# First norm of batches 3 to 7 from x loaded channels first, its factors by way of DRAM; first and last group norm by halves, spread by TensorE; new turns

## The chip, the core and the metric

The kernel runs on one NeuronCore of a Trainium2 chip. Its engines are TensorE (PE in the profile; its weight loads are PEld), VectorE (DVE), ScalarE (ACT), GpSimd (POOL) and SyncE (SP), which here only issues DMAs. The metric is the device time of one execution in microseconds; less is better.

## What is computed

One RWKV block over x of 8 batches, 256 tokens and 512 channels, all in float32, cut to what matters here:

```python
xn = ln(x, ln1_w, ln1_b)                      # first norm, over the 512 channels of a token
sx = shift(xn) - xn                           # the token before, less the token itself
xxx = tanh((xn + sx * maa_x) @ maa_w1)        # 5 groups of 32
x5 = xn + sx * (maa + xxx @ maa_w2)           # five mixtures
w = exp(-exp(time_decay + tanh(x5[1] @ decay_w1) @ decay_w2))
r, k, v = x5[3] @ Wr.T, x5[0] @ Wk.T, x5[2] @ Wv.T
g = silu(x5[4] @ Wg.T)
for t in tokens:                              # 32 heads of 16 x 16
    a = k[t][:, None] * v[t][None, :]
    out[t] = r[t] @ (u * a + s)
    s = a + w[t][:, None] * s
att = group_norm(out) * gn_w + gn_b           # over the 16 channels of a head
x = x + (att * g) @ Wo.T
xn2 = ln(x, ln2_w, ln2_b); sx2 = shift(xn2) - xn2
xk, xr = xn2 + sx2 * ffn_maa_k, xn2 + sx2 * ffn_maa_r
out = x + sigmoid(xr @ ffn_Wr.T) * (square(relu(xk @ ffn_Wk.T)) @ ffn_Wv.T)
```

## The kernel before

Each batch passes three stages: `inputs_of_scan` (first norm, mixtures, projections k, v, r, g), `scan` (the recurrence, one scan instruction of VectorE over 4 x 256 elements, 16 of them a batch) and `rest` (group norm, Wo, second norm, feed-forward). Activations lie channels first: 128 channels by 256 tokens, two such blocks to a tile.

`Plan` records every operation with an engine, a guessed duration and its buffers, and `order` lays them out: an operation with a lower rank goes first where it can start. The ranks are the table `TURNS` (lines 127 to 263), one row for each stage of each batch; `LANDS`, `WAY` and the others are guesses of DMA times that enter the layout only. What reaches the chip is a fixed order of instructions on each engine. All loads and stores but those of v go out on SP's queue in that order, and an instruction that waits holds up all behind it on its queue.

Names that matter:

- The first norm of batches 2 to 7 (`normed`, lines 592 to 641): two ScalarE passes over each of two token tiles sum x and its squares (L595, L599), GpSimd makes the factor by a power (L634), ScalarE scales the tile (L638), and `turned` has TensorE turn it in 8 transposes (L658) into PSUM, from where ScalarE applies the weight and bias (L681). GpSimd takes the shift difference `sx` (L690).
- The scan (`scan`): v goes to DRAM (`vo`) and comes back spread over partitions (`vs<-vo`, 128 DMAs of 512 KB into 6 buffers), is multiplied by k (L1001, or on GpSimd L998), scanned (L1003, into `st`), multiplied by r on GpSimd (L1006) and summed over partitions by TensorE (L1014, "the gather", 16 matmuls of a quarter of the array's columns each).
- The group norm (`rest`, lines 1029 to 1086): squares (L1032), means of squares by four matmuls (L1040, into a quarter of the columns each), a square root (L1045), a reciprocal on VectorE (L1051). For batches 0 to 6 the 32 rows that result are spread to 128 partitions by 16 ScalarE copies (L1073), and GpSimd multiplies (L1076); for batch 7 TensorE spreads them (L1059) and VectorE multiplies (L1067). Then weight and bias (L1080), the gate (L1085 or L1083) and Wo.
- The second norm of batches 0 to 6 makes its mixtures with `between`: two scaled copies on ScalarE (L729, L734), added on GpSimd (L736).
- ScalarE's functions lie in sets; `tables` puts a table load (L1170) where the next function is not in the set that is loaded.
- TensorE instructions come in forms: the full array ("128*128"), a quarter of the columns ("128*32", four side by side), a quarter or a half of the rows ("32*128", "64*128"), and transposes. Where several are side by side, one row of the profile holds them all.

```python
act(256, rs, [pv, eh], lambda: nc.scalar.activation(
    rs()[:, 0:T], pv()[:, 0, :], AF.Sqrt, bias=eh()[:, 0:1]), "sqrt", 1)
...
    dve(256, [rs], [rs], lambda: nc.vector.reciprocal(rs()[:, 0:T], rs()[:, 0:T]), 6.25)
```

Of the kernel before, what the change touches and what calls it, by code (L numbers as in the profile page):

```python
# [12 lines left out]
P = 128  # L13
# [55 lines left out]
class Plan:  # L69
# [5 lines left out]
    LANDS = {"vs__": (2.3, 2.45), "s": (0.3, 2.4), "vo_": (0.7, 2.2), "vo__": (0.35, 2.0), "o_": (0.7, 1.2), "x": (1.8, 2.3),  # L75
             "xt": (1.7, 2.0), "xs": (0.7, 0.9), "idt": (0.2, 1.6), "Wfk_": (1.7, 2.7), "Wfr_": (1.7, 2.7),
             "Wfv_": (1.7, 2.7), "Wo_": (1.7, 2.7)}
    WAY = 1.4
    TABLES = {"exp": "exp_and_others", "tanh": "exp_and_others", "silu": "silu_and_others", "sig": "sigmoid_and_others",
              "sqrt": "sqrt_and_others"}  # L80
# [16 lines left out]
    def add(self, engine, us, outs, ins, emit, mode=None, into=(), lag=0.0, kb=0, part=False):  # L97
# [3 lines left out]
        if kb:  # L101
            op.wire, op.lag = self.LANDS.get("".join(c for c in op.bufs[0].name if not c.isdigit()), (kb / 308, 1.7))

# [17 lines left out]
    def stage(self):  # L121
# [258 lines left out]
def tile_rwkv_block(  # L380
# [133 lines left out]
    def load(buf, src, kb):  # L514
        dma(buf, lambda: src, buf, kb)
# [730 lines left out]
```

## Time and profile before

| | |
|---|---|
| median of 3 runs | 608.0 us (607.12 to 609.82) |
| span of the profiled execution | 607.4 us |
| busy: DVE | 539.7 us (89%) |
| busy: ACT | 519.0 us (85%) |
| busy: POOL | 511.6 us (84%) |
| moved by DMA | 124.73 MB, mean 205 GB/s |

The profile shows one execution and gives no time of its own but the span, from the first to the last instruction; the median of the runs lies 0.6 us above it. Busy times are sums over an engine's instructions, shares are of the span. A row of groups names line, engine, operation, tiles out and in, count, then busy time, mean length of one, and the idle time just before, with what ended it. A row of a window gives its length, each engine's busy time with its instructions, and the clock granted to TensorE as a share of full speed.

### The profile page before, as it was taken

How to read it: one execution, taken by the hardware profiler on the slowest of the kernel's cores; microseconds unless marked ns; L12 is line 12 of the kernel's file. 1: busy time of each engine (PE TensorE's matmuls, PEld its weight loads, DVE VectorE, ACT ScalarE, POOL GpSimd, SP SyncE). 2: the span in 40 equal slices, each digit the busy share in tenths (PEclk: the TensorE clock that was granted, in tenths of full speed). 3: DMA queues.
4: the chain of work that ended last, by engine and by line, in shares of the span. 5: the costliest groups of instructions: out<-in, count | busy, mean ns of one | idle time of the engine just before them, and what ended most of it. 6: DMA issues, size and time to landing. Idle time of an engine off the chain costs nothing.

```text
span 607.4 us, 17029 instructions
## 1 busy us (share of the span) xinstructions
PE 596.5 (98%) x7022; PEld 346.3 (57%) x7022; DVE 539.7 (89%) x492; ACT 519.0 (85%) x1177; POOL 511.6 (84%) x405
## 2 busy tenths in 40 slices
PE   9999998899999999999999999999999999999997
PEld 7575655347634774446654584465744474546464
DVE  5789999799999999998899999999899999995342
ACT  5977879979999999989999999999998899968350
POOL 2989999989979999899989899988889798987020
PEclk9999999799999999999999999999999999999999
DMA  9887695649668789669767987788667878972352
GB/s 316 272 198 209 184 253 170 167 119 284 193 162 227 198 250 244 182 191 253 202 196 214 269 215 213 210 256 216 166 184 195 231 202 216 282 206 74 130 187 77
DMA packets 52638, 124.73 MB, mean 205 GB/s; under 512 B 5841, under 2 KB 11345, under 8 KB 52561
## 3 DMA queue, kind: packets, MB, share of 16 engines
q1 hardware_dynamic: 48048, 119.39, 70.3%
q10 hardware_dynamic: 4512, 4.26, 2.2%
q8 instruction: 55, 0.90, 0.7%
q14 instruction: 23, 0.18, 0.1%
HBM read 115.25 MB, written 8.39 MB: 204 GB/s over the span
## 4 chain that ended last, share of the span: by engine, by line
PE 68%; POOL 14%; ACT 7%; DVE 5%; DMA 3%; issue 2%; SPq 0%; ACTq 0%; DVEq 0%; POOLq 0%
PE ps L440 57%; POOL st L1006 7%; PE ps L1014 7%; POOL mix L822 3%; PE ps L658 2%; POOL vs L998 1%; DVE st L1003 1%; DMA vo<-v 1%; PE ps L862 1%; PE ps L564 1%; DMA x<-in_x 1%; DMA vs<-vo 1%; DVE vs L1001 1%; ACT xh L595 1%; POOL mix L850 1%
## 5 line engine op out<-in xcount | busy, mean ns | idle before, releaser
L1003 DVE TENSOR_TENSOR_SCAN st<-wrep,vs 128x1024 f32<-128x1024 f32 x128 | 287.9, 2273 | 7.1 <-PE ps L1014 3.5
L1006 POOL TENSOR_TENSOR st<-st,r 128x1024 f32<-128x1024 f32 x128 | 254.8, 2008 | 7.4 <-DVE st L1003 6.0
L1001 DVE TENSOR_TENSOR vs<-vs,ps 128x1020 f32<-128x1020 f32 x122 | 142.6, 1199 | 2.0 <-ACT ps L980 1.0
L440 PE MATMUL ps<-Ws,mix 128*32 128x512 f32 (+3 forms) x872 | 115.1, 585 | 0.0
L440 PEld LDWEIGHTS ps<-Ws,mix 128*32 128x32 f32 (+1 forms) x872 | 37.5, 116 | 63.1 <-issue 58.5
L822 POOL TENSOR_TENSOR mix<-mix,xn 128x512 f32<-128x512 f32 x62 | 66.9, 1103 | 4.1 <-DVE mix L806 4.0
L1014 PE MATMUL ps<-st,con 128*32 128x256 f32 x1024 | 63.7, 388 | 2.4 <-POOL st L1006 1.6
L440 PE MATMUL ps<-mix,Wv 128*32 128x256 f32 (+1 forms) x832 | 59.5, 380 | 1.2 <-DVE mix L819 1.0
L440 PE MATMUL ps<-mix,Wk 128*32 128x256 f32 (+1 forms) x856 | 59.8, 380 | 0.0
L440 PE MATMUL ps<-mix,Wr 128*32 128x256 f32 (+1 forms) x712 | 59.2, 380 | 0.0
L440 PE MATMUL ps<-mix,Wg 128*32 128x256 f32 (+1 forms) x544 | 58.1, 380 | 0.1
L440 PE MATMUL ps<-Ws,g 128*32 128x512 f32 (+1 forms) x416 | 58.1, 606 | 0.0
L440 PE MATMUL ps<-mix,Ws 128*32 128x256 f32 (+1 forms) x688 | 57.8, 380 | 0.0
L1014 PEld LDWEIGHTS ps<-st,con 128*32 128x32 f32 x1024 | 33.1, 111 | 30.0 <-issue 9.0
L440 PEld LDWEIGHTS ps<-mix,Wg 128*32 128x32 f32 (+1 forms) x544 | 42.2, 133 | 12.8 <-issue 0.7
L440 PEld LDWEIGHTS ps<-mix,Wv 128*32 128x32 f32 (+1 forms) x832 | 36.6, 116 | 22.4 <-issue 3.0
L440 PEld LDWEIGHTS ps<-mix,Ws 128*32 128x32 f32 (+1 forms) x688 | 39.6, 123 | 16.7 <-issue 1.4
L440 PEld LDWEIGHTS ps<-mix,Wr 128*32 128x32 f32 (+1 forms) x712 | 38.8, 122 | 16.9 <-issue 1.3
L440 PEld LDWEIGHTS ps<-mix,Wk 128*32 128x32 f32 (+1 forms) x856 | 37.0, 115 | 19.8 <-issue 2.2
L804 ACT ACTIVATE ps<-ps,vec 128x256 f32<-128x256 f32 x112 | 45.5, 448 | 2.9 <-PE ps L440 2.0
L1170 ACT ACT_TABLE_LOAD x33 | 42.3, 1283 | 0.6
L736 POOL TENSOR_TENSOR mix<-mix,sx 128x512 f32<-128x512 f32 x28 | 35.5, 1279 | 6.6 <-ACT mix L729 3.7
(143 smaller groups left out, 1000.4 us busy)
## 6 DMA issues: line engine op xcount, KB each, us to landing
vs<-vo SPq DMA_DIRECT2D x128, 512.0 KB, 5.2
Ws<-in_wo SPq DMA_DIRECT2D x16, 512.0 KB, 5.4
Ws<-in_fk SPq DMA_DIRECT2D x16, 512.0 KB, 5.5
Ws<-in_fr SPq DMA_DIRECT2D x16, 512.0 KB, 5.7
Ws<-in_fv SPq DMA_DIRECT2D x16, 512.0 KB, 5.3
x<-in_x SPq DMA_DIRECT2D x9, 512.0 KB, 6.0
vo<-v ACTq DMA_DIRECT2D x15, 256.0 KB, 5.4
out<-o SPq DMA_DIRECT2D x15, 256.0 KB, 3.8
```

The lines of the kernel that those rows point to most:

```text
L440: nc.tensor.matmul(out[i : i + n], lhsT=w[:, i : i + n], rhs=x, start=first, stop=final)
L564: nc.tensor.matmul(ps()[:, 0, :], lhsT=warm[:, 0, 0:P], rhs=warm[:, 0, 0:T], start=True, stop=True)
L595: summed(junk[n], mv, [src[n]], lambda n=n: nc.scalar.activation(junk[n](), src[n](), AF.Copy, accum_out=mv()[:, n, 0:1]), 0)
L658: nc.tensor.transpose(to[:, m, n * P : (n + 1) * P], xh[n]()[:, k * P : (k + 1) * P], idt())
L736: gp(512, t, [t, u], lambda t=t, u=u: nc.gpsimd.tensor_tensor(t(), t(), u(), ALU.add))
L804: act(256, p_, [p_, vec], lambda g=g, q=q, m=m, p_=p_: nc.scalar.activation(p_()[:, m, :], p_()[:, m, :], AF.Identity, bias=col(f"maa_{g}" ...
L822: gp(512, t, [t, xn[q]], lambda q=q, t=t: nc.gpsimd.tensor_tensor(t(), t(), xn[q]()[:, :, 1 : T + 1], ALU.add))
L1001: dve(4 * T, [vs], [vs, kp], lambda m=m, vs=vs, kp=kp: nc.vector.tensor_tensor(vs()[:, :, 1:T], vs()[:, :, 1:T], kp()[:, m : m + 1, 1:T].t ...
L1003: dve(4 * T, [st], [w, vs, first], lambda w=w, vs=vs, st=st: nc.vector.tensor_tensor_scan(st().rearrange("p n t -> p (n t)"), w().rearrang ...
L1006: gp(4 * T, st, [st, r], lambda m=m, st=st, r=r: nc.gpsimd.tensor_tensor(st(), st(), r()[:, m : m + 1, :].to_broadcast([P, 4, T]), ALU.mul ...
L1014: nc.tensor.matmul(pat()[32 * i : 32 * i + 32, 0, :], lhsT=con()[:, s : s + 32], rhs=done[i]()[:, j, :], start=(j == 0), stop=(j == 3),)
L1170: nc.scalar.preload_act_table_set(op.table)
```

## The change

- **First norm of batches 3 to 7.** The host passes x a second time with channels first (`x_turned`). The sums over x stay as they were. GpSimd makes the factor and minus mean times factor (`rn`), one DMA writes these 2 x 256 numbers to DRAM (`bd`), one reads them back spread over all 128 partitions (`bc`). ScalarE copies the factor row into PSUM, two DMAs bring x channels first straight into `xn`, VectorE multiplies, GpSimd adds, ScalarE applies weight and bias in place. The two scalings L638, the 8 transposes and their way out of PSUM are gone for these batches.
- **Group norm.** Square root and reciprocal become a logarithm and an exponential of -1/2 of it, both on ScalarE, in one set of functions that other exponentials may use too. In batches 0 and 7 each half of the channels has its own means, logarithm, exponential and spreading by TensorE, and VectorE multiplies; so batch 0 loses its 16 copies and both GpSimd multiplications.
- **Smaller.** The second scaled copy of `between` lies one element further in its tile. The weights `mw2b` and `dw2` are passed without repeats.
- **Turns.** All ranks and the guesses of DMA times are new.

```diff
-    LANDS = {"vs__": (2.3, 2.45), "s": (0.3, 2.4), "vo_": (0.7, 2.2), "vo__": (0.35, 2.0), "o_": (0.7, 1.2), "x": (1.8, 2.3),
...
-    WAY = 1.4
+    LANDS = {"vs__": 2.33, "s": 0.4, "vo_": 0.85, "vo__": 0.25, "o_": 0.8, "x": 1.55, "xt": 1.5, "xs": 0.9, "idt": 0.2,
...
+    WAY, LANDED = 1.18, 1.15
-              "sqrt": "sqrt_and_others"}
+              "sqrt": "sqrt_and_others", "ln": "natural_log_exp_and_others"}
...
     TURNS = """
-        8 72 12 20 41 124 40 135 48 116 79 78 141 119 3 32 84 31 128 181 183 185 11 10 19 39 62 68 36 65 69 37
+        8 80 3 54 31 46 105 114 69 103 123 75 126 116 1 4 27 113 106 108 111 112 33 5 41 49 52 53 34 45 73 43
...
+            elif want == "exp" and mode == "ln":
+                want = mode
...
+        "sx": lambda t: t[:, 0 : 2 * T].rearrange("p (m t) -> p m t", m=2),
...
+        spread = which == 1 and b > 2
...
+        if spread:
+            return turned_by_host(mn, rs, row, b)
...
+    def turned_by_host(mn, rs, row, b):
+        u, i = f"1_{b}", NVEC + 2 * b + row
+        rn, there, bc, rsb = new("rn", f"rn{b}"), new("bd", f"bd_{b}"), new("bc", f"bc{b}"), new("ps", f"rsb{b}")
+        gp(2, rn, [rs, eh], lambda: nc.gpsimd.tensor_tensor(rn()[:, 0, :], rs(), eh()[:, 2:4], ALU.pow), 340)
+        gp(2, rn, [mn, rn], lambda: nc.gpsimd.tensor_tensor(rn()[:, 1, :], mn(), rn()[:, 0, :], ALU.mult), 30)
+        dma(there, lambda: rn(), lambda: there().rearrange("w (n p) -> p w n", p=P), 2, rn)
+        dma(bc, lambda: there().unsqueeze(0).to_broadcast([P, 2, T]), bc, 262, there)
+        act(256, rsb, [bc], lambda: nc.scalar.copy(rsb()[:, 0, :], bc()[:, 0, :]))
+        xns, sxs = [], []
+        for q in range(NQ):
+            xn, sx = new("xn", f"xn{u}_{q}"), new("sx", f"sx{u}_{q}")
+            dma(xn, lambda q=q: x_turned[b, 2 * q * P : (2 * q + 2) * P, :].rearrange("(m p) t -> p m t", p=P),
+                lambda xn=xn: xn()[:, :, 1 : T + 1], 262)
...
+            dve(512, [xn], [xn, rsb], lambda xn=xn: nc.vector.tensor_tensor(
+                xn()[:, :, 1 : T + 1], xn()[:, :, 1 : T + 1], rsb()[:, 0:1, :].to_broadcast([P, 2, T]), ALU.mult))
+            gp(512, xn, [xn, bc], lambda xn=xn: nc.gpsimd.tensor_tensor(
+                xn()[:, :, 1 : T + 1], xn()[:, :, 1 : T + 1], bc()[:, 1:2, :].to_broadcast([P, 2, T]), ALU.add))
+            for m in range(2):
+                k = 2 * q + m
+                act(256, xn, [xn, vec], lambda m=m, k=k, xn=xn: nc.scalar.activation(
+                    xn()[:, m, 1 : T + 1], xn()[:, m, 1 : T + 1], AF.Identity, bias=col("ln1_b", k), scale=col("ln1_w", k)), pointers=2)
...
-            u = new("sx", f"u{name}_{q}")
+            u = Buf("sx", f"u{name}_{q}", lambda t: t[:, 1 : 2 * T + 1].rearrange("p (m t) -> p m t", m=2))
...
+        split = b == 0 or last
+        if split:
+            pr = []
+            for q, sq in enumerate(sqs):
+                pv, half = new("ps", f"pv{b}_{q}"), slice(64 * q, 64 * q + 64)
...
+                pe(0.437, [pv], [con, sq], mm, "columns")
+                act(256, sq, [pv, eh], lambda sq=sq, pv=pv, half=half: nc.scalar.activation(
+                    sq()[half, 0:T], pv()[half, 0, :], AF.Ln, bias=eh()[half, 0:1]), "ln", 1)
+                act(256, sq, [sq], lambda sq=sq, half=half: nc.scalar.activation(
+                    sq()[half, 0:T], sq()[half, 0:T], AF.Exp, scale=-0.5), "ln")
+                p_ = new("ps", f"psr{b}_{q}")
...
+                        nc.tensor.matmul(p_()[:, m, :], lhsT=con()[half, s : s + P], rhs=sq()[half, 0:T], start=True, stop=True)
...
-            dve(256, [rs], [rs], lambda: nc.vector.reciprocal(rs()[:, 0:T], rs()[:, 0:T]), 6.25)
...
+            act(256, rs, [rs], lambda: nc.scalar.activation(rs()[:, 0:T], rs()[:, 0:T], AF.Exp, scale=-0.5), "ln")
```

How the order of instructions moves is shown at three places. A row gives line, operation and tiles (`_` and a number is the buffer), then the shape of the output.

The first place is GpSimd around the gate of batch 0's group norm. Before, the last of 20 products `st` of the scan stands behind the two multiplications by the spread factors (`att<-att,sq` and `att<-att,rk`), and the gate (`g<-att,g`) behind that:

```order
L998 TENSOR_TENSOR vs_149<-vs_149,k_127 128x4x255
L1006 TENSOR_TENSOR st_156<-st_156,r_128 128x1024
L1006 TENSOR_TENSOR st_159<-st_159,r_128 128x1024
L1076 TENSOR_TENSOR att_141<-att_141,sq_162 128x2x256
L1076 TENSOR_TENSOR att_142<-att_142,rk_153 128x2x256
L1006 TENSOR_TENSOR st_155<-st_155,r_128 128x1024
L1085 TENSOR_TENSOR g_138<-att_141,g_138 128x512
L1085 TENSOR_TENSOR g_137<-att_142,g_137 128x512
```

Now the gate of one half stands ahead of the last four of the same 20 products and that of the other just behind them:

```order
L1137 TENSOR_TENSOR g_140<-att_143,g_140 128x512
L1047 TENSOR_TENSOR st_162<-st_162,r_132 128x1024
L863 TENSOR_TENSOR mix_117<-mix_117,xn_105 128x512
L863 TENSOR_TENSOR mix_119<-mix_119,xn_104 128x512
L1047 TENSOR_TENSOR st_160<-st_160,r_132 128x1024
L1039 TENSOR_TENSOR vs_152<-vs_152,k_129 128x4x255
L1047 TENSOR_TENSOR st_164<-st_164,r_132 128x1024
L1047 TENSOR_TENSOR st_161<-st_161,r_132 128x1024
L1137 TENSOR_TENSOR g_139<-att_144,g_139 128x512
```

The two multiplications are gone from GpSimd, and the gates have moved ahead; the kinds of work up to the 20th product are otherwise the same in number.

The second place is TensorE where batch 0's group norm takes its means. Before, both halves of the squares (`sq`) go in together, and nothing of the norm follows on this engine:

```order
L440 MATMUL ps_175<-mix_113,Wv_78 32x256 x8
L440 MATMUL ps_175<-mix_121,Wv_79 32x256 x8
L1040 MATMUL ps_174<-sq_161,con 32x256 x2
L1040 MATMUL ps_174<-sq_162,con 32x256 x2
L862 MATMUL ps_173<-mix_117,dw_69 32x256 x2
```

Now one half comes alone, and its spreading follows after half a projection:

```order
L447 MATMUL ps_181<-mix_121,Wr_81 32x256 x8
L1085 MATMUL ps_182<-sq_166,con 32x256 x2
L447 MATMUL ps_180<-mix_123,Wr_80 32x256 x8
L447 MATMUL ps_180<-mix_121,Wr_81 32x256 x8
L1098 MATMUL ps_182<-sq_166,con 128x256 x2
L447 MATMUL ps_177<-ta_125,mw2a 128x256
```

Two of the four matmuls for the means and two new ones of half the rows stand by themselves; the other half follows in the same way further on. Over the whole kernel transposes fall from 128 to 88, and the places where TensorE passes from one form to another from 108 to 93.

The third place is SP's queue where the factors of batch 3's first norm pass through DRAM. Before there is nothing of the kind. Now the write (`bd`) waits for GpSimd, the read (`bc`) for the write, and loads of the scan (`vs`) and of weights (`Ws`) stand between and behind:

```order
L436 DMA s_84<-in_state 128x64
L436 DMA bd_149<-rn_101 128x4x1
L436 DMA vs_157<-vo_146 128x1x1024
L436 DMA bc_151<-bd_149 128x512
L436 DMA Ws_172<-in_fr 128x2x512
L436 DMA vs_153<-vo_146 128x1x1024
L436 DMA vs_154<-vo_146 128x1x1024
```

One load of the scan stands between the write and the read, and the loads behind the read now wait for it.

More of the change, by code (lines that the diff above doesn't have):

```diff
@@ L101, in add @@
         if kb:
-            op.wire, op.lag = self.LANDS.get("".join(c for c in op.bufs[0].name if not c.isdigit()), (kb / 308, 1.7))
+            op.wire = self.LANDS.get("".join(c for c in op.bufs[0].name if not c.isdigit()), kb / 308)
+            op.lag = self.LANDED
         op.bufs += [b for b in into if b not in op.bufs]
@@ L317, in order @@
                     mode["ACT"] = now = want
+                elif want == "exp" and now == "ln":
+                    want = now
             if want and want != now:
@@ L383, in tile_rwkv_block @@
     x: bass.AP,
+    x_turned: bass.AP,
     vecs: bass.AP,
@@ L388, in tile_rwkv_block @@
     maa_w2: bass.AP,
+    maa_w2_last: bass.AP,
     decay_w1: bass.AP,
@@ L452, in tile_rwkv_block @@
     idt, con, vec = const("idt", [P, P]), const("con", [P, NCONST - P]), const("vec", [P, NK, NVEC + 2 * NB])
-    w1, w2a, w2b = const("mw1", [P, NK, 6 * MAA]), const("mw2a", [P, E]), const("mw2b", [P, E])
-    dw1, dw2 = const("dw1", [P, NK, DEC]), const("dw2", [2 * DEC, E])
+    w1, w2a, w2b = const("mw1", [P, NK, 6 * MAA]), const("mw2a", [P, E]), const("mw2b", [P, P])
+    dw1, dw2 = const("dw1", [P, NK, DEC]), const("dw2", [2 * DEC, 2 * P])
     hm = const("hm", [P, NK, 32])
@@ L469, in tile_rwkv_block @@
     pool("nm", 2, [P, NT])
+    pool("rn", 2, [P, 2, NT])
     pool("xn", 4, [P, 2, T + 1])
-    pool("sx", 4, [P, 2, T])
+    pool("sx", 4, [P, 2 * T + 2])
     pool("mix", 14, [P, 2, T])
@@ L482, in tile_rwkv_block @@
     pool("vo", 3, [2, P, T], dram)
+    pool("bd", 2, [2, T], dram)
+    pool("bc", 1, [P, 2, T])
     pool("vs", 6, [P, 4, T])
@@ L835, in mm @@
                     rows = slice(k * MAA, (k + 1) * MAA)
-                    mul(ps[k]()[:, 0, :], w2b()[rows, k * P : (k + 1) * P], tb()[rows, :], tiles=False)
+                    mul(ps[k]()[:, 0, :], w2b()[rows, :], tb()[rows, :], tiles=False)
             pe(0.52, ps, [tb, w2b], mm, "rows32", ts)
@@ L885, in mm @@
                 for q in range(NQ):
-                    rows, k = slice(DEC * q, DEC * q + DEC), 2 * q + m
-                    mul(pw[q]()[:, m, :], dw2()[rows, k * P : (k + 1) * P], hd()[rows, 1, :], tiles=False)
+                    rows = slice(DEC * q, DEC * q + DEC)
+                    mul(pw[q]()[:, m, :], dw2()[rows, m * P : (m + 1) * P], hd()[rows, 1, :], tiles=False)
         pe(0.945, pw, [dw2, hd], mm, "rows64", ws)
@@ L1034, in rest @@
             sqs.append(sq)
-        pv, rs = new("ps", f"pv{b}"), sqs[0]
-        def mm():
-            for blk in range(NK):
-                rows = slice(32 * blk, 32 * blk + 32)
-                nc.tensor.matmul(
-                    pv()[rows, 0, :], lhsT=con()[:, C_MEAN : C_MEAN + 32], rhs=sqs[blk // 2]()[:, blk % 2 * T : blk % 2 * T + T],
-                    start=True, stop=True)
-        pe(0.437, [pv], [con, *sqs], mm, "columns")
-        act(256, rs, [pv, eh], lambda: nc.scalar.activation(
-            rs()[:, 0:T], pv()[:, 0, :], AF.Sqrt, bias=eh()[:, 0:1]), "sqrt", 1)
@@ L1047, in rest, with mm @@
-        kept = False
-        if kept:
-            dve(256, [pv], [rs], lambda: nc.vector.reciprocal(pv()[:, 0, :], rs()[:, 0:T]), 6.25)
-        else:
-            dve(256, [rs], [rs], lambda: nc.vector.reciprocal(rs()[:, 0:T], rs()[:, 0:T]), 6.25)
-        if last:
-            pr = [new("ps", f"psr{b}_{q}") for q in range(NQ)]
+        split = b == 0 or last
[3 more added lines that the diff above has]
+                pv, half = new("ps", f"pv{b}_{q}"), slice(64 * q, 64 * q + 64)
+                def mm(q=q, sq=sq, pv=pv):
+                    for m in range(2):
+                        rows = slice(64 * q + 32 * m, 64 * q + 32 * m + 32)
+                        nc.tensor.matmul(pv()[rows, 0, :], lhsT=con()[:, C_MEAN : C_MEAN + 32], rhs=sq()[:, m * T : m * T + T],
+                                         start=True, stop=True)
+                pe(0.437, [pv], [con, sq], mm, "columns")
[4 more added lines that the diff above has]
+                p_ = new("ps", f"psr{b}_{q}")
+                def mm(sq=sq, p_=p_, half=half):
+                    for m in range(2):
+                        s = C_SEL + m * P
+                        nc.tensor.matmul(p_()[:, m, :], lhsT=con()[half, s : s + P], rhs=sq()[half, 0:T], start=True, stop=True)
+                pe(0.864, [p_], [con, sq], mm, "rows64")
+                pr.append(p_)
+        else:
+            pv, rs = new("ps", f"pv{b}"), sqs[0]
@@ L1055, in mm @@
             def mm():
-                for m in range(2):
-                    for q in range(NQ):
-                        rows, s = slice(64 * q, 64 * q + 64), C_SEL + m * P
-                        nc.tensor.matmul(
-                            pr[q]()[:, m, :], lhsT=con()[rows, s : s + P], rhs=rs()[rows, 0:T], start=True, stop=True)
-            pe(0.945, pr, [con, rs], mm, "rows64")
+                for blk in range(NK):
+                    rows = slice(32 * blk, 32 * blk + 32)
+                    nc.tensor.matmul(
+                        pv()[rows, 0, :], lhsT=con()[:, C_MEAN : C_MEAN + 32], rhs=sqs[blk // 2]()[:, blk % 2 * T : blk % 2 * T + T],
+                        start=True, stop=True)
@@ L1063, in rest @@
+            pe(0.437, [pv], [con, *sqs], mm, "columns")
+            act(256, rs, [pv, eh], lambda: nc.scalar.activation(
+                rs()[:, 0:T], pv()[:, 0, :], AF.Ln, bias=eh()[:, 0:1]), "ln", 1)
+            act(256, rs, [rs], lambda: nc.scalar.activation(rs()[:, 0:T], rs()[:, 0:T], AF.Exp, scale=-0.5), "ln")
         ys = []
@@ L1065, in rest @@
             att, g = got["att", q], got["g", q]
-            if last:
+            if split:
                 dve(512, [att], [pr[q], att], lambda att=att, ps=pr[q]: nc.vector.tensor_tensor(att(), ps(), att(), ALU.mult))
@@ L1072, in rest @@
                         rows = slice(32 * i, 32 * i + 32)
-                        act(335 if kept else 376, rsb, [pv if kept else rs], lambda blk=2 * q + n, n=n, rows=rows, rsb=rsb: nc.scalar.copy(
-                            by_block(rsb)[rows, n, :],
-                            (pv()[:, 0, :] if kept else rs()[:, 0:T])[32 * blk : 32 * blk + 32, :]))
+                        act(376, rsb, [rs], lambda blk=2 * q + n, n=n, rows=rows, rsb=rsb: nc.scalar.copy(
+                            by_block(rsb)[rows, n, :], rs()[32 * blk : 32 * blk + 32, 0:T]))
                 gp(512, att, [att, rsb], lambda att=att, rsb=rsb: nc.gpsimd.tensor_tensor(
@@ L1145, in tile_rwkv_block @@
     load(w1, maa_w1.rearrange("(k p) j -> p k j", p=P), 384)
-    load(w2a, maa_w2[0:4].rearrange("g j e -> (g j) e"), 256)
-    load(w2b, maa_w2[4:].rearrange("g j e -> (g j) e"), 256)
+    load(w2a, maa_w2, 256)
+    load(w2b, maa_w2_last, 64)
     load(dw1, decay_w1.rearrange("(k p) j -> p k j", p=P), 128)
-    load(dw2, decay_w2, 256)
+    load(dw2, decay_w2, 128)
     for n, src in (("k", wk), ("r", wr), ("g", wg)):
@@ L1218 @@
         "x": x,
+        "x_turned": x.transpose(0, 2, 1),
         "vecs": vecs,
@@ L1222 @@
         "maa_w1": np.concatenate([w1, w1[:, 4 * MAA :]], axis=1),
-        "maa_w2": np.concatenate([a["maa_w2"], *[a["maa_w2"][4:]] * (3)], axis=0),
+        "maa_w2": a["maa_w2"][:4].reshape(4 * MAA, E),
+        "maa_w2_last": np.concatenate([a["maa_w2"][4][:, k * P : (k + 1) * P] for k in range(NK)], axis=0),
         "decay_w1": a["decay_w1"],
-        "decay_w2": np.concatenate([by_channel(a["decay_w2"].T).T] * 2, axis=0),
+        "decay_w2": np.concatenate(np.split(by_channel(a["decay_w2"].T).T, NQ, axis=1), axis=0),
         "wk": by_channel(a["Wk"]).T,
```

10 lines of the change are left out of this document (8 added, 2 removed), and 267 rows, old and new, of the table TURNS.

## The prediction

> **What bounds the kernel.** The page's busy times come first, then its chain of work that ended last:
>
> ```profile
> span 607.4 us, 17029 instructions
> PE 596.5 (98%) x7022; PEld 346.3 (57%) x7022; DVE 539.7 (89%) x492; ACT 519.0 (85%) x1177; POOL 511.6 (84%) x405
> PE 68%; POOL 14%; ACT 7%; DVE 5%; DMA 3%; issue 2%; SPq 0%; ACTq 0%; DVEq 0%; POOLq 0%
> ```
>
> TensorE is busy nearly throughout, but GpSimd holds 14% of the chain. A cut into stages (length, busy time of PE, PEld, DVE, ACT and POOL, granted clock, DMA share, GB/s) shows where:
>
> ```profile
> 38.00:97.00 59.00, 57.97 (x1013) 34.72 (x1015) 58.15 (x51) 47.14 (x100) 58.30 (x39) 1.00 0.80 210
> 97.00:112.70 15.70, 14.67 (x270) 8.39 (x262) 15.35 (x11) 13.98 (x31) 15.70 (x12) 1.00 0.48 137
> 112.70:116.30 3.60, 0.83 (x16) 0.36 (x15) 2.58 (x3) 3.57 (x9) 3.60 (x4) 0.88 1.01 261
> 116.30:119.70 3.40, 3.40 (x36) 1.56 (x40) 0.85 (x2) 3.35 (x9) 3.40 (x3) 0.50 1.05 248
> 119.70:127.80 8.10, 8.10 (x68) 2.13 (x64) 6.84 (x6) 5.79 (x14) 8.10 (x6) 0.84 0.71 182
> 127.80:555.70 427.90, 427.75 (x5108) 245.39 (x5100) 412.31 (x336) 397.90 (x919) 391.46 (x300) 1.00 0.76 211
> ```
>
> From 127.8 to 555.7 us TensorE loses 0.15 us: whatever leaves its own queue there is gained whole, and the others have 15.6 (DVE), 30.0 (ACT) and 36.4 us (POOL) to spare. The one real loss lies around batch 0's group norm. There TensorE idles 1.03 and 2.77 us, 3.8 together, and then its clock is halved: 0.12 x 3.6 + 0.50 x 3.4 + 0.16 x 8.1 = 3.4 us of full speed lost. Whom it waits for is in the chain of waits, read between 108 and 120 us, and in the list of TensorE's waits:
>
> ```profile
> 108.18 3.98 POOL st L1006 x2
> 112.16 2.09 POOL att L1076 x2
> 114.25 1.97 POOL st L1006
> 116.26 3.64 PE ps L1014 x32
> PE ps L1014 <- POOL st L1006: 1.6, 1, 1.6
> ```
>
> The gather at 116.26 waits for the last product, which stands behind the two multiplications L1076; at half clock the gather takes 3.64 us.
>
> **TensorE's own work.** The chain's pieces give the price of a turning and of a passage between forms:
>
> ```profile
> 331.31 1.73 PE ps L1014 x32
> 346.81 1.02 PE ps L658 x8
> 349.56 1.86 PE ps L1014 x32
> 364.77 0.87 PE ps L658 x8
> 381.55 0.48 PE ps L1040 x8
> ```
>
> 1. Transposes: eight in a group take 0.87 us; 128 become 88, so five groups go: 5 x 0.87 = **-4.35**.
> 2. A passage costs 1.86 - 1.73 = 0.13 on a gather and 1.02 - 0.87 = 0.15 on transposes; 108 - 93 = 15 fewer at 0.14: **-2.1**.
> 3. Halves. A gather is four matmuls side by side, four times over: 1.73 / 4 = 0.43 a place. The means of a norm fill one place (0.48 with the passage); each half alone takes one place as well, so a split norm has 0.43 more. For the spreading the tail shows the halves side by side, and the mean of one matmul:
>
> ```profile
> 563.24 1.06 PE ps L1059 x8
> L1059 PE MATMUL ps<-sq,con 64*128 64x256 f32 x8 | 1.1, 402 | 0.0
> ```
>
> Four matmuls alone are four places, 1.73 us. Batch 7 gains 1.73 - 1.06 + 0.43 = **+1.1**. Batch 0 gains 1.73 + 0.43 = 2.1, where TensorE idled 3.8; I count nothing, as this fills idle time, with 2.1 if that cover is gone. The low end is 0, if lone halves pair with neighbours after all; the high end 3.2. From means to spreading a half now takes a logarithm and an exponential where a root and a reciprocal stood (1.74 against about 0.47, rows below), so I count no new wait in the tail.
>
> **The head.** GpSimd up to the 20th product loses two L1076 (2.09 us) and takes in one gate of the shape of one of them, 2.09 / 2 = 1.05, so the gather can start 1.05 sooner, at 115.2. TensorE without its 3.8 of waits and with 2.1 more work would arrive at 116.26 - 3.8 + 2.1 = 114.6. It then waits 0.6 us instead of 3.8. Did the clock fall because of the wait? In the stage before, with 1.03 us idle in 15.70, it stayed at 1.00; it fell where 2.77 of 3.60 were idle. So I take it to hold: -1.05 - 3.4 = **-4.5**; the ends are -1.05 (the clock halves again) and -3.8 - 3.4 + 2.1 = -5.1.
>
> The Trainium skill, page "TensorE: Matmul & The Clock Gate", section "HAM oscillation — how this bites in real kernels", gives as its rule to have no idle gaps over about 3.4 us. The longest gap here was 1.6 us and the clock halved all the same, so the measurement decides. By the rule the clock's fall would not be due to the gap, and the sum would keep 3.4 us more, as in the first rival.
>
> **The other engines**, which have room, so none of this enters the sum:
>
> ```profile
> L1051 DVE RECIPROCAL sq<-sq 128x256 f32<-128x256 f32 x8 | 13.9, 1736 | 2.5 <-ACT sq L1045 2.5
> L806 DVE TENSOR_TENSOR mix<-ps,sx 128x512 f32<-128x512 f32 x56 | 36.1, 675 | 1.0 <-ACT ps L804 0.7
> L638 ACT ACTIVATE xh<-xt,nm,rs 128x512 f32<-128x512 f32 x12 | 9.6, 819 | 0.0
> L1073 ACT COPY rk<-sq 32x256 f32<-32x256 f32 x56 | 22.5, 402 | 1.3 <-ACT v L901 0.4
> L1045 ACT ACTIVATE sq<-ps,eh 128x256 f32<-128x256 f32 x8 | 3.8, 474 | 0.3 <-PE ps L1040 0.3
> L1170 ACT ACT_TABLE_LOAD x33 | 42.3, 1283 | 0.6
> L822 POOL TENSOR_TENSOR mix<-mix,xn 128x512 f32<-128x512 f32 x62 | 66.9, 1103 | 4.1 <-DVE mix L806 4.0
> L736 POOL TENSOR_TENSOR mix<-mix,sx 128x512 f32<-128x512 f32 x28 | 35.5, 1279 | 6.6 <-ACT mix L729 3.7
> ```
>
> VectorE loses 8 reciprocals of 1.74 and gains 10 products from PSUM and two for batch 0's spread at 0.68: -5.8 us. ScalarE loses 10 scalings of 0.82 and 16 copies of 0.40, gains 10 exponentials and two more logarithms of 0.47, five copies at 0.40 and a table load of 1.28: -5.7. GpSimd gains 10 adds of 1.10, loses two multiplications of 1.10, and 28 adds of L736 have an operand moved by one element. Those take 1279 ns where L822 takes 1103 and has one operand so shifted; 28 x 0.176 = -4.9 if the alignment is the reason, 0 if not. So GpSimd stands between +3.9 and +8.8, in 36.4 of room. Where these covers fail is the next term.
>
> **New waits.** Fewer microseconds on TensorE leave the others less room: VectorE is busy 412.3 less its share of 5.8, against some 421. Bounds: 0.15, as the stretch lost before; and the rate of 38 to 97 us, where VectorE and GpSimd were both at 99%: 1.03 / 59 x 421 = 7.3. VectorE here is at 97%, nearer to the first: **+1.5**. Whether GpSimd is late for a mixture is in this too.
>
> **The path by DRAM.** For each of five batches there are one write of 2 KB, one read of 256 KB, and two loads of 256 KB of x beside the one for the sums. These rows are nearest:
>
> ```profile
> vs<-vo SPq DMA_DIRECT2D x128, 512.0 KB, 5.2
> DMA to landing us min/median/max: 4.2/5.2/10.7
> out<-sq SPq DMA_DIRECT2D x1, 64.0 KB, 1.5
> L1001 DVE TENSOR_TENSOR vs<-vs,ps 128x1020 f32<-128x1020 f32 x122 | 142.6, 1199 | 2.0 <-ACT ps L980 1.0
> L1003 DVE TENSOR_TENSOR_SCAN st<-wrep,vs 128x1024 f32<-128x1024 f32 x128 | 287.9, 2273 | 7.1 <-PE ps L1014 3.5
> ```
>
> SP's queue holds the read until the write has landed: 1.5 to 10.7 us, and the scan's loads stand behind. Six buffers hold 6 x (1.20 + 2.27) = 20.8 us of VectorE's work; less a landing of 5.2 and the step in hand of 3.5, SP may stand still for 12.1 us before VectorE runs dry. The ends leave it inside, so 0 in the sum, the other end being the second rival. The DMA share of 0.76 leaves room for five times 0.77 MB in 124.73 MB.
>
> The Trainium skill, page "DMA: Bandwidth & Descriptors", section "Rules for kernel authors", says that a strided last dimension becomes one descriptor per element. The write scatters 512 numbers of 4 bytes, and no run here shows such a write; by the page it would stand nearer the long end than its 2 KB suggest.
>
> **Sum**, against the profiled execution: 607.4 - 4.35 - 2.1 + 1.1 - 4.5 + 1.5 = 599.05 us. The median of the runs lies 0.6 above the span: **599.6**.
>
> **Rivals.** 0.5%, 3.0 us, is about what a measurement of this kernel can tell from no change, so faster means below 605.0 and slower above 611.0.
>
> - *The head stays.* Batch 0's spreading needs a logarithm, an exponential and two passes by TensorE in a row; if it delays TensorE instead of filling, the gather starts only 1.05 sooner and the clock halves again: 599.6 + 3.4 = 603.0. For it: GpSimd stays the chain there. Against: the idle share falls from 77% to under 20%. Chance 0.14.
> - *VectorE or GpSimd becomes the bound* in the long stretch: 7.3 instead of 1.5, 605.4. For it: GpSimd takes in work that TensorE and ScalarE drop, and the turns are new. Against: 15 and 36 us of room. Chance 0.12.
> - *Slower: the round trip by DRAM stops the scan.* SP stands for 15 us, VectorE runs dry for 3, and five batches give 5 x 3 = +15, 599.6 + 15 = 614.6. It decides from 12.1 us, and passes 611 from 14.4. For it: 10.7 us have been seen for one landing, and the factors on GpSimd come ahead of it. Against: the median is 5.2. Chance 0.12.
> - The forecast: 0.62. Its own range is from 599.6 - 1.1 (halves at 0) - 1.5 (no new waits) - 0.6 (the head's low end) = 596.4, less 0.9 for the runs' spread below their median, to 599.6 + 2.1 (batch 0's cover gone) + 1.8 (their spread above), so 595 to 603.5.
>
> The range takes in the first two rivals, the second with the same 2.1 and 1.8 on top (609.3), and leaves out the third: **595 to 609**. Faster holds the forecast and 0.10 of the first rival, whose 603.0 lies near the bound: 0.72. The same holds its other 0.04, the second, and 0.01 of the third: 0.17. Slower is the rest of the third: 0.11.
>
> **What would show it.** Right: 88 transposes; no reciprocal of 128x256; around the fifth gather and the first Wo a granted clock of 1.00, under 1 us idle, and a gather of 1.8 us, not 3.6; in the long stretch under 2 us of idle on TensorE; the add of `between` near 1.10. Wrong: a clock of 0.5 at that gather; TensorE's waits there naming `mix` from GpSimd or `st` from VectorE; VectorE waiting for `vs` from DMA just behind a `bc`. A tail that got longer than before by more than 1 us would speak against the third term.

## The result, and the profile after

The changed kernel takes 644.4 us (median of 4 runs, 643.0 to 648.6) against 607.6 for the kernel before in the same runs: a ratio of 1.062 (95% interval 1.058 to 1.067). It is 6.2% slower, outside the range, on the side to which the third rival pointed. The page's span, busy times and chain of the changed kernel:

```profile
span 641.2 us, 18588 instructions
PE 599.0 (93%) x7770; PEld 336.2 (52%) x7770; DVE 538.5 (84%) x496; ACT 517.7 (81%) x1169; POOL 517.2 (81%) x413
PE 59%; ACT 13%; DMA 12%; POOL 7%; DVE 5%; issue 3%; SPq 0%; ACTq 0%; DVEq 0%; POOLq 0%
```

No engine has over 1.1% more to do than before, yet all are idle for longer, and DMA has gone from 3% to 12% of the chain. A cut of its program into stages (columns as above) tells where TensorE stands idle:

```profile
118.00:165.00 47.00, 36.16 (x412) 22.20 (x416) 34.78 (x29) 33.55 (x83) 35.27 (x29) 0.93 0.64 156
165.00:214.00 49.00, 48.65 (x688) 25.37 (x680) 48.30 (x41) 47.31 (x107) 46.02 (x36) 1.00 0.75 206
214.00:262.00 48.00, 41.06 (x536) 24.43 (x540) 37.91 (x31) 36.11 (x84) 37.15 (x31) 0.93 0.79 178
287.00:312.00 25.00, 20.76 (x288) 12.82 (x284) 15.71 (x16) 17.84 (x46) 18.59 (x17) 0.93 0.73 159
369.00:425.00 56.00, 50.89 (x756) 26.24 (x752) 50.52 (x45) 49.43 (x121) 50.13 (x43) 1.00 0.83 190
126.75:136.20 9.45, 6.96 (x108) 3.68 (x104) 9.10 (x8) 5.61 (x17) 4.67 (x4) 1.00 0.13 19
```

TensorE idles for 10.8, 6.9, 4.2 and 5.1 us in the four poor stages, with the clock down in three. The first three of them hold one write `bd` each, the fourth holds two; the second row, a stage without one, loses 0.35. The last row is the time from just behind the first of these writes to the read `bc`: the 16 DMA engines move 19 GB/s, a tenth of the usual. Behind the second write they move 26 GB/s; behind the other three, where loads issued earlier were still under way, 78, 119 and 187. SP's timeline there, in order of issue (start, length, what):

```profile
118.42 0.58 SPq L436 DMA_DIRECT2D s<-in_state  x1
125.44 0.38 SPq L436 DMA_DIRECT2D bd<-rn  x1
125.98 0.53 SPq L436 DMA_DIRECT2D vs<-vo  x1
136.19 0.34 SPq L436 DMA_DIRECT2D bc<-bd  x1
136.63 0.38 SPq L436 DMA_DIRECT2D Ws<-in_fr  x1
```

SP waits 6.4 us for `rn` and then 9.7 for the write to land, with one load sent between. The DMA rows (KB each, median us to landing):

```profile
vs<-vo SPq DMA_DIRECT2D x128, 512.0 KB, 6.4
bc<-bd SPq DMA_DIRECT2D x5, 256.0 KB, 9.1
bd<-rn SPq DMA_DIRECT2D x5, 2.0 KB, 12.6
```

The 12.6 of `bd` is one landing, the only one of the five that the trace tells; behind all five writes the read that waits for them goes out 10.2 to 12.6 us later. From 125 to 127 us, the packets of the DMA view, and the landing of the load sent right behind the write:

```profile
DMA packets 528, 0.00 MB, mean 1 GB/s; under 512 B 528, under 2 KB 528, under 8 KB 528
vs<-vo SPq DMA_DIRECT2D x1, 512.0 KB, 15.0
```

The write's packets are all out within two microseconds; that it has landed is told some ten later. The load behind it, which SP did not hold, lands after 15.0 us, where the median of before was 5.2. Three readings are open here. SP may be what starves the loads, as it stands still; the write may slow the transfers behind it; or the new turns may leave no cover at all.

### The profile page after: what moved, and what is told of

Same layout as the page of the kernel before. It is cut to its first block, busy times and chain, and to the rows that moved or that the text cites. A ratio compares the mean times of both kernels' runs of the same rounds, so it can differ in the third digit from the quotient of the medians.

```text
span 641.2 us, 18588 instructions
## 1 busy us (share of the span) xinstructions
PE 599.0 (93%) x7770; PEld 336.2 (52%) x7770; DVE 538.5 (84%) x496; ACT 517.7 (81%) x1169; POOL 517.2 (81%) x413
## 4 chain that ended last, share of the span: by engine, by line
PE 59%; ACT 13%; DMA 12%; POOL 7%; DVE 5%; issue 3%; SPq 0%; ACTq 0%; DVEq 0%; POOLq 0%
PE ps L447 51%; DMA vs<-vo 8%; PE ps L1055 5%; POOL st L1047 3%; DVE st L1044 2%; ACT L1222 2%; PE ps L903 2%; DMA Ws<-in_fv 1%; POOL mix L863 1%; DMA xn<-in_x_turned 1%; PE ps L671 1%; ACT ps L845 1%; ACT vs L1035 1%; DVE vs L1042 1%; ACT wrep L1023 1%
## 5 line engine op out<-in xcount | busy, mean ns | idle before, releaser
L447 PEld LDWEIGHTS ps<-Ws,mix 128*32 128x32 f32 (+1 forms) x860 | 39.6, 117 | 63.1 <-issue 54.3
L447 PE MATMUL ps<-mix,Wk 128*32 128x256 f32 (+1 forms) x1000 | 61.3, 387 | 7.8 <-ACT w L934 7.0
L447 PE MATMUL ps<-mix,Ws 128*32 128x256 f32 (+1 forms) x928 | 60.3, 387 | 7.6 <-DVE att L1061 3.2
L447 PE MATMUL ps<-mix,Wv 128*32 128x256 f32 (+1 forms) x880 | 61.3, 386 | 6.2 <-issue 4.2
L1035 ACT ACTIVATE vs<-s,cm 128x4 f32<-128x4 f32 x128 | 35.5, 296 | 23.7 <-DMA vs<-vo 23.0
L447 PEld LDWEIGHTS ps<-mix,Ws 128*32 128x32 f32 (+1 forms) x928 | 37.1, 115 | 29.9 <-issue 3.7
L1055 PEld LDWEIGHTS ps<-st,con 128*32 128x32 f32 x1024 | 34.5, 110 | 32.7 <-issue 9.8
L447 PEld LDWEIGHTS ps<-mix,Wk 128*32 128x32 f32 (+1 forms) x1000 | 33.8, 112 | 31.5 <-ACT w L934 7.4
L447 PEld LDWEIGHTS ps<-mix,Wg 128*32 128x32 f32 (+1 forms) x760 | 37.8, 119 | 19.9 <-issue 2.6
```

The lines of the kernel that those rows point to most:

```text
L447: nc.tensor.matmul(out[i : i + n], lhsT=w[:, i : i + n], rhs=x, start=first, stop=final)
L1035: plan.add("ACT", 0.19336, [first], [s0, cm, landed], lambda i=i, blk=blk, vs=vs: nc.scalar.activation(vs()[:, :, 0:1], s0()[:, blk, 4 * i ...
L1055: nc.tensor.matmul(pat()[32 * i : 32 * i + 32, 0, :], lhsT=con()[:, s : s + 32], rhs=done[i]()[:, j, :], start=(j == 0), stop=(j == 3),)
```

## The experiments

**The read freed, then both freed.** `bc` reads a part of `x_turned`, so SP no longer waits for the write; then `bd` writes a constant as well.

```diff
-        dma(bc, lambda: there().unsqueeze(0).to_broadcast([P, 2, T]), bc, 262, there)
+        dma(bc, lambda: x_turned[b, 0:2, :].unsqueeze(0).to_broadcast([P, 2, T]), bc, 262, there)
```

> The spread read `bc` takes its numbers from `x_turned` and so no longer waits for the write `bd`; order, sizes and number of all transfers stay (the factors written by `bd` are not used, so the first norm of batches 3 to 7 is left without them). Theory W (SP stands still for the write, 9.6 us at batch 3 and 26.5 us in all, and the loads of the scan behind it come late): most of the 36 us go, 604 to 618 us, the rest being the wait for `rn` (7.2 us) in front of `bd`. Theory T (the added traffic and the 512 small descriptors of each `bd` slow the loads): nothing changes, 638 to 648. Theory O (the new turns leave no cover on GpSimd and VectorE): nothing changes, 638 to 648.

> As the run before, and `bd` writes a constant instead of `rn`, so that SP waits neither for GpSimd's factors nor for the write; order, sizes and number of all transfers stay. Theory W: 597 to 606 us, TensorE idle under 6 us between 40 and 580 us, and if the gap behind batch 0's products is gone as forecast, a granted clock of 1.00 there. Theory T: 636 to 648, since the same bytes and descriptors move. Theory O: 636 to 648.

Measured: 639.5 us (ratio 1.053, 1.047 to 1.059) and 630.9 (1.039, 1.035 to 1.043). The first fits theories T and O alike, the second lies between all of its forecasts. SP's waits, taken away one and both, give back 5 and 13 us of 37, so theory W holds for the smaller part at most. With the read free, the window behind batch 3's write reads:

```profile
126.00:136.00 10.00, 10.00 (x132) 4.78 (x127) 9.66 (x9) 8.67 (x23) 6.91 (x6) 1.00 0.15 17
```

SP waits for nothing there and the loads are issued; still only 17 GB/s move. That points to the write itself.

**The shape of the write.** The same 512 numbers go out as 128 runs of 16 bytes, as 256 runs of 8, singly with 64 bytes between them, and singly with 16. In the last two the read is free as above.

```diff
-        dma(there, lambda: rn(), lambda: there().rearrange("w (n p) -> p w n", p=P), 2, rn)
+        dma(there, lambda: rn(), lambda: there().rearrange("w (a b n) -> (w a) b n", b=2, n=2), 2, rn)
```

```diff
-    pool("bd", 2, [2, T], dram)
+    pool("bd", 2, [2, T, 16], dram)
...
+        dma(there, lambda: rn(), lambda: there()[:, :, 0].rearrange("w (n p) -> p w n", p=P), 2, rn)
```

> `bd` writes its 512 numbers as 128 runs of 16 bytes in place of 512 of 4 bytes (so the factors come back in another order and the norm of batches 3 to 7 is off); all waits stay. If the write's landing (7 to 13 us) comes from its number of descriptors, it falls to 3 to 5 us and the time by 15 to 25 us, to 618 to 628. If it comes from the queue of large loads ahead of it, landing and time stay, 638 to 648.

> `bd` writes runs of two numbers: 256 runs of 8 bytes, between the change's 512 of 4 and the 128 of 16 of the run before (two tokens change places, so the factors of batches 3 to 7 fall on wrong tokens); all waits stay. Theory N (each short run costs about 18 ns, one after the other, and until they are through the loads behind them trickle): the write lands 2.5 + 256 x 0.018 = about 5 to 7 us after its issue, and the time is 615 to 628. If only runs of 4 bytes are slow: landing and time as with 16-byte runs, 606 to 614.

> As the run in which the read is freed of its wait (639 us), but each of the 512 numbers of `bd` goes 64 bytes from the next, so no two share 64 bytes of DRAM (the read takes `x_turned`, the factors are not used). Theory N (the count of runs is what costs): 632 to 646, landing near 12 us. Theory S (writes that fall on the same 64 bytes wait for one another): landing under 7 us and 604 to 616.

> As the run with 64 bytes between the numbers (613 us), but 16 bytes between them: 512 writes of 4 bytes, four to each 64 bytes of DRAM, as many as with the 128 runs of 16 bytes laid closely (read freed, factors not used). Theory S (what counts is how many writes fall on the same 64 bytes): landing of `bd` 4 to 7 us and 608 to 616, near the run of 16-byte runs. If neighbouring writes collide over more than 64 bytes: landing over 9 us and 622 or more.

| write of 512 numbers | writes to each 64 bytes | landing of `bd`, us | time, us |
|---|---|---|---|
| 4 bytes, packed, read free | 16 | 11.7 | 639.5 |
| 8-byte runs, packed | 8 | 6.1 | 614.1 |
| 16-byte runs, packed | 4 | 4.7 | 610.6 |
| 4 bytes, 16 apart, read free | 4 | 5.4 | 610.7 |
| 4 bytes, 64 apart, read free | 1 | 4.8 | 613.1 |

Times of the last four are single runs, and the first landing is that of one write. The others are medians of five: their single landings run from 1.4 to 7.7 us, and those of the 8-byte runs, 3.9 to 7.4, don't stand out. The row of the window behind the write, with 64 bytes between the numbers:

```profile
126.00:136.00 10.00, 10.00 (x144) 5.28 (x140) 9.66 (x9) 9.77 (x26) 9.76 (x10) 1.00 0.90 218
```

218 GB/s with as many writes of 4 bytes as at 17 GB/s. The 16-byte runs came out 7 us below what I expected of them. The 8-byte runs came out 1 us below theory N's range and at the upper edge of its rival's. That the number of runs costs (theory N) falls with the spaced writes. What counts is how close together the writes fall. The 64 bytes of the table are a way of counting: by 16 or 32 bytes the packed single numbers stand highest as well, so the size within which writes collide isn't shown.

**The waits once the write is quick.** 16-byte runs, with nothing for SP to wait for:

> 128 runs of 16 bytes, and neither `bd` nor `bc` waits for what goes ahead (a constant is written, `x_turned` is read, so the factors are not used); same bytes and order. If the waits of SP cost something of their own once the write is quick: 600 to 605 us against 610.6 with them. If they cost nothing: 607 to 612.

610.1 us (1.006, 1.004 to 1.008), as with the waits (610.6): then they cost nothing. This run and the one with both freed (630.9) differ in the shape of the write alone, so 21 us of the loss are the write's with no wait of SP in play. All runs with a quick write have the new turns, so these are not what costs the 37 us.

**The write by itself.** Five such writes are put into the kernel before, ahead of a load of the scan; nobody reads them or waits for them. Once they are packed and once 64 bytes apart, `[2, T, 1]` and `[2, T, 16]`:

```diff
+        if b in scattered and blk == 0 and i == 0:
+            nc.sync.dma_start(out=scattered[b][:, :, 0].rearrange("w (n p) -> p w n", p=P), in_=eh().rearrange("p (w n) -> p w n", w=2))
```

> The kernel before, and on SP's queue, ahead of the first load of the scan of batches 2 to 6, one write of 512 numbers of 4 bytes to a closely packed 2 KB of DRAM (a constant, read by nobody; nothing waits for it, all else stands as before). If such a write holds up the loads behind it by some 9 us each time, whatever the turns: 12 to 35 us more, 618 to 642. If it hurts only in the changed kernel's order, where loads come late already: under 4 us more, up to 610.

> The same five writes, but 64 bytes between the numbers. Theory S (writes that fall on the same 64 bytes of DRAM wait for one another): 0 to 4 us more than the kernel before, up to 610. If the number of small writes costs by itself: as the run with packed writes.

Packed: 621.6 us (ratio 1.024, 1.019 to 1.029), so 14.5 more, 2.9 for each write. Apart: 606.3 (0.999, 0.997 to 1.001), the same. The landings of the writes, packed (one write) and then apart (median of five), and what VectorE waits for with the packed ones:

```profile
bd<-eh SPq DMA_DIRECT2D x5, 2.0 KB, 11.3
```

```profile
bd<-eh SPq DMA_DIRECT2D x5, 2.0 KB, 5.8
```

```profile
DVE vs L1007 <- DMA vs<-vo: 17.8, 9, 4.0
```

This is the cause by itself, in an order that is otherwise that of before: VectorE waits for these loads once, for 0.8 us, in the kernel before and with the writes apart; with the packed ones it waits nine times.

**The old norm in the new turns.**

> First norm of batches 3 to 7 as before (scalings, 8 transposes each, no DRAM), with the turns of the changed kernel carried over to the operations that correspond; all else of the change stays. Theories W and T: near the kernel before, 600 to 612 us, as both put the loss on the path by DRAM. Theory O: 630 to 648, with TensorE's waits spread over many tiles and SP not among them.

681.2 us (1.125, 1.120 to 1.131), slower than all. The turns carried over belong to other operations, and TensorE's transposes waited for ScalarE, 8.8 us of it for the scalings; the run says nothing on the turns themselves.

**The change with a quick write.** Here nothing is left out: 16-byte runs, and ScalarE's copy and GpSimd's add fetch the factors by a stride; then the same with the copy of `between` moved back by one element.

```diff
+        def row_of(w):
+            return bc().rearrange("q w t -> q (w t)").rearrange("q (p w n) -> q w n p", p=P, w=2)[:, w]
...
-            u = Buf("sx", f"u{name}_{q}", lambda t: t[:, 1 : 2 * T + 1].rearrange("p (m t) -> p m t", m=2))
+            u = Buf("sx", f"u{name}_{q}", lambda t: t[:, 0 : 2 * T].rearrange("p (m t) -> p m t", m=2))
```

> The change with the write in 128 runs of 16 bytes, and ScalarE's copy and GpSimd's add reading the factors back in their places by a stride; nothing is left out. Theory N: as with the runs of 16 bytes, 606 to 613 us, so within 1% of the kernel before; strided reading costs GpSimd up to 10 x 0.2 us and TensorE nothing. If strided reading doubles the add (1.18 to 2.4 us): 614 to 624.

> The corrected change (612.1 us) with the second scaled copy of `between` at its old place, one element back. By the prediction GpSimd's 28 adds go from 1.09 back to 1.28 us, 5.3 us in all, covered: the same time, 610.5 to 614. If GpSimd has become the bound in the long stretch: 4 to 6 us more, 616 to 618.

612.1 us (1.010, 1.008 to 1.013) and 616.4 (1.016, 1.013 to 1.020). So even mended, the change doesn't beat the kernel before. By the medians 5.5 us more of GpSimd's adds cost some 4, as the second forecast had it; but the two intervals touch, and of the two executions profiled the one without the shift was the shorter (613.8 against 614.6). That the adds aren't covered is likely and not shown. GpSimd's groups, with the shift and then without:

```profile
L782 POOL TENSOR_TENSOR mix<-mix,sx 128x512 f32<-128x512 f32 x28 | 30.3, 1090 | 0.4
L729 POOL TENSOR_TENSOR xn<-xn,bc 128x512 f32<-128x512 f32 x10 | 15.6, 1579 | 1.2 <-issue 0.6 <-DVE xn L727 0.5
```

```profile
L782 POOL TENSOR_TENSOR mix<-mix,sx 128x512 f32<-128x512 f32 x28 | 35.8, 1288 | 0.1
```

**The head alone, in the kernel before.** Batch 0 is spread by TensorE and multiplied on VectorE; all other instructions keep their order. Then with the products, weights and gates as early as they can stand, and last with a logarithm and an exponential of ScalarE in place of root and reciprocal.

```diff
-        if last:
+        wide = last or b == 0
+        if wide:
             pr = [new("ps", f"psr{b}_{q}") for q in range(NQ)]
```

> The kernel before with one part of the change alone: batch 0's group norm is spread by TensorE (both halves together, as batch 7's is there) and multiplied on VectorE, so GpSimd loses its two multiplications and ScalarE its 16 copies; all else stands in the order of before, and nothing is left out. By the prediction's fourth step (the two multiplications hold up the fifth gather, and the idle time makes the clock fall): the gather starts 1.5 to 2.1 us sooner, the granted clock stays at 1.00, and the time is 3 to 5.5 us less, 601 to 603.5 against 606.4. By its first rival (the clock falls all the same): 604.3 to 606. If the new logarithm-free spreading stands in TensorE's way: 606.4 or more.

> The kernel before with batch 0's spreading by TensorE as in the run that came out at 609.6, but its products on VectorE, its weights and its gates now stand as early as they can; nothing is left out. There VectorE was busy throughout from 38 to 112 us, the products came behind two pairs of scans, the gate was 1.1 us late for the gather and the clock fell all the same. If only that late place was at fault: 602 to 605. If VectorE is the bound of this stage, so that two products (1.3 us) on it cost what they take, whatever GpSimd saves: 606 to 608.5.

> As the run beside it, and batch 0's root and reciprocal (1.73 us of VectorE) become a logarithm and an exponential of ScalarE, with one table load more; all other batches as before. If VectorE is the bound of the stage: 1.0 to 2.0 us less than the run beside it, 604 to 607. If not (GpSimd alone, as the prediction had it): the same as the run beside it, within 0.7 us.

609.6 us (1.005, 1.003 to 1.008), 609.5 (1.005, 1.003 to 1.006) and 607.0 (1.002, 1.000 to 1.003). The first run's stages around the norm, and the chain's pieces in front of its fifth gather:

```profile
38.00:97.00 59.00, 57.82 (x1018) 34.63 (x1016) 59.00 (x51) 47.73 (x100) 59.00 (x41) 1.00 0.82 205
97.00:112.70 15.70, 12.01 (x200) 7.49 (x204) 15.70 (x11) 7.00 (x15) 15.42 (x11) 1.00 0.66 184
```

```profile
118.64 0.42 DVE mix L847
119.06 0.14 DVE cm L943
119.20 0.01 issue
119.21 3.57 PE ps L1016 x32
```

VectorE is busy without a break from 38 to 112.7 us, and stands last ahead of the gather, which comes 3 us later than before where 1.5 to 2.1 sooner was expected. The half clock (3.57 us) is not what makes this run longer: in five of its eight executions the clock held at 1.000, and they took 609.2 to 609.7 us. The same gather in the last run:

```profile
116.37 1.93 PE L1016 MATMUL ps<-st,con 128*32 128x256 f32 x32 [1.46 <-DVE cm L943]
```

Less work for GpSimd gained nothing while VectorE got two products more, and an early place for them didn't help: the second run lies above both of its forecasts. 1.73 us less of VectorE gave back 2.5, a little over what was expected. No version made here beats the kernel before.

## Why the prediction was wrong, point by point

**The step that failed is "the path by DRAM".** It put the write at nothing, since SP might stand still for 12.1 us and a landing takes 1.5 to 10.7. The third rival had the place and the sign, and gave 15 us at 0.12; but its mechanism, SP held between write and read, is the smaller one: freeing the read alone left 639.5. In its place the runs show that a write of 512 single numbers to a packed 2 KB slows the transfers behind it for some 10 us, whether SP waits or not: written in 16-byte runs, the same numbers give back some 34 of the 37 us. The sign that the prediction named for this, VectorE waiting for `vs`, showed, with 9.2 us. The landing taken as nearest, of 64 KB in long rows (1.5 us), says nothing on such a write, and the 12.1 us of grace hold only if the loads behind it land in their usual 5.2 us, not in 15.0.

The Trainium skill's rule in "DMA: Bandwidth & Descriptors", section "Rules for kernel authors", one descriptor for each element, agrees with the 528 packets for 512 numbers. The same page of the Trainium skill, section "Specifications", says that transfers under 512 bytes go by read, modify and write; no run here shows that step. Number and size alone cost nothing here: spaced by 64 bytes, the same writes left the kernel before at 606.3 us.

**TensorE's own work (terms 1 to 3) came out as a sum.** With 16-byte runs, where the clock stays up, it is busy 590.4 us, and 590.3 to 593.2 in the other runs with a quick write. Forecast: 596.5 less 3.4 for the clock, 4.35 for the transposes and 2.1 for the passages, and 1.1 and 2.1 more for the halves: 589.85. No run measures a passage or a lone half by itself. The groups of the changed kernel show the 88 transposes:

```profile
L671 PE MATMUL ps<-idt,xh 128*128 128x128 f32 x88 | 12.7, 281 | 1.4 <-ACT xh L651 1.0 <-DVE xh L639 0.4
```

**The head (term 4) was half right.** In the execution profiled with 16-byte runs the fifth gather takes 1.93 us and not 3.64. The idle pieces in front of it are 0.71 and 1.07 us, where they were 1.17 and 1.59:

```profile
118.91 1.93 PE L1055 MATMUL ps<-st,con 128*32 128x256 f32 x32 [1.07 <-DVE mix L886]
```

But the gather comes at 118.9, not at 115.2: without GpSimd's two multiplications it is no sooner, as in the runs on the head alone. The profile of before had VectorE busy for 58.15 of 59.00 and 15.35 of 15.70 us beside GpSimd, and I followed the one engine that the chain named.

Nor are the clock's 3.4 us a loss of every execution. Of the 69 executions of the kernel before that ran beside the experiments in under 610 us, 27 have a mean granted clock of 1.000 (median 605.4 us), 35 have 0.996 or 0.997 (606.7), and 7 have 0.994 (608.0), as the profiled one has. The mean lies 0.0022 below 1; of some 605 us that is, as an estimate, 1.3 us lost on the average and not 3.4. The forecast took the price from one of the worst executions.

**New waits (term 5) were mis-sized.** The stages of the kernel before, and of the one with 16-byte runs:

```profile
0.00:20.00 20.00, 17.68 (x114) 14.54 (x118) 13.30 (x34) 12.43 (x28) 8.24 (x24) 1.00 0.95 337
20.00:120.00 100.00, 95.18 (x1508) 58.22 (x1512) 90.03 (x85) 84.42 (x189) 97.39 (x72) 0.98 0.74 198
120.00:560.00 440.00, 439.86 (x5244) 249.85 (x5240) 419.54 (x343) 406.39 (x934) 401.77 (x307) 1.00 0.76 209
```

```profile
0.00:20.00 20.00, 15.21 (x126) 11.99 (x126) 12.03 (x31) 11.87 (x29) 7.05 (x22) 1.00 0.93 322
20.00:120.00 100.00, 96.07 (x1469) 59.81 (x1465) 91.48 (x88) 80.67 (x177) 95.86 (x72) 1.00 0.82 208
120.00:560.00 440.00, 435.46 (x6040) 236.28 (x6036) 417.90 (x348) 408.65 (x940) 408.80 (x317) 1.00 0.80 214
```

TensorE's idle time goes from 2.3 to 4.8 us in the first stage, from 4.8 to 3.9 in the second and from 0.1 to 4.5 in the third. Behind 560 us it goes from 3.6 (47.4 less 43.81) to 5.0 (48.7 less 43.66). Forecast were 3.2 less at the head and 1.5 more in the stretch; the 2.5 at the start and 1.4 at the end had no step at all. At the start TensorE waits 1.44 us for a load (`Ws<-in_consts`) that SP now issues at 3.55 us and not at 2.10, as the turns there are new too. At the end it waits 1.44 us for VectorE. The waits, then the products of VectorE before and after:

```profile
8.68 3.81 PE L447 MATMUL ps<-Ws,Ws 128*128 128x128 f32 x32 [1.44 <-DMA Ws<-in_consts]
584.95 6.74 PE L447 MATMUL ps<-mix,Ws 128*128 128x256 f32 x30 [1.44 <-DVE mix L752]
```

```profile
L711 DVE SCALAR_TENSOR_TENSOR mix<-sx,vec,xn 128x256 f32<-128x256 f32 x4 | 1.7, 476 | 0.0
L752 DVE SCALAR_TENSOR_TENSOR mix<-sx,vec,xn 128x256 f32<-128x256 f32 x4 | 3.3, 896 | 0.0
```

The same four products of the last second norm take 1.7 us more in all. They read `sx`, whose tile has two numbers more in the changed kernel; whether that is the reason wasn't tested. So the tail did get longer, from 51.7 us behind the start of the last gather to 53.3, past the 1 us that was to speak against the third term; but the wait is for these products and not for the halves. The other engines lost less work than was counted: with 16-byte runs VectorE is busy 1.7 us less than before and ScalarE 2.4, where 5.8 and 5.7 were forecast, and GpSimd 4.7 more, inside the range forecast. The room of 36 us on GpSimd was a sum over 428 us, and such a sum doesn't tell whether the room is there when it is needed. Which of the turns costs the 4.4 us of the long stretch stays open.

The term of +0.6 between span and run was small as well: in the runs after, both are known for the same execution, and lie 1.8 apart (643.0 and 641.2).

## What to carry to other kernels

A short detour by DRAM is judged by the pattern of its write, not by its bytes: 2 KB in packed single words held back megabytes, and the same words in runs of 16 bytes, or spaced out, held back nothing that could be measured. Take away the wait and the traffic separately before you believe that a queue was the cause. And where two engines are busy without a break, as here, taking work off the one in the chain gained nothing when it was handed to the other. Last, a loss that one profile shows is priced by how often other executions of the same kernel show it.

## What the runs showed of the hardware

- 512 writes of 4 bytes to a packed 2 KB have landed after 10.2 to 12.6 us, and behind the first of them in the changed kernel the DMA engines move 17 to 19 GB/s until then. With 8 writes to each 64 bytes the median landing is 6.1 us, with 4 or fewer 4.7 to 6.5. That they wait for one another at the memory fits these numbers; where, wasn't shown.
- While the third write is out, TensorE stands for 4.2 us and the profile names nothing that it waits for:

```profile
299.32 2.79 PE L447 MATMUL ps<-mix,Wv 128*32 128x256 f32 x23 [4.24 <-issue]
```

  Its waits of this kind come to 6.9 us, and to none in the run with 16-byte runs. The page lists a DMA queue for instructions, with 61 packets. That such packets were held back would fit; it wasn't tested.
- GpSimd's add of 128 x 512 takes 1.288 us with both operands at the start of their tiles, and 1.090 with one of them an element further on. Reading an operand by a stride of four numbers takes 1.579 against 1.185.
- The granted clock of the same kernel differs between executions: 1.000 in 27 of 69, 0.994 to 0.997 in the others, with medians of 605.4 and 606.7 to 608.0 us.
